# A two-hop graph diffusion: pieces of side work woven between half products instead of whole ones

## The chip, the core and the metric

The kernel runs on one core of a Trainium2 chip. The metric is device time in microseconds. The time of the kernel before is the median of three runs; the profile is of one more execution.

## The reference

Two layers follow each other, each with a pre-norm (`h = relu(layernorm(x))`) and a residual sum. The first is a graph attention over 4096 nodes, 256 features and 4 heads. The second, which the change concerns, is a diffusion of two steps with two ways of mixing nodes:

```python
R = S + I;  R = R / R.sum(-1)              # S is the 4096 x 4096 adjacency
Z = 0;  Xf = X;  Xa = X                    # X is 4096 x 256
for n in range(2):
    q = Xa @ W1.T @ W2.T;  k = Xa @ W3.T   # 64 wide
    probs = softmax(q @ k.T)               # 4096 x 4096
    # per row: keep the largest probs until their sum reaches 0.9, renormalise
    A = probs * mask / (probs * mask).sum(-1)
    Xf = R @ Xf                            # one "hop" over the graph
    Xa = A @ Xa                            # top-p attention
    Z = Z + Xf @ U1[n].T + Xa @ U2[n].T
out = x + layernorm(X + Z)
```

All of it is float32.

## The kernel before

Blocks have 128 nodes, so there are 32 of them (`NB`). After layer 0 (to about 838 us of the span) come, for step 0 and then for step 1: a **hop**, which multiplies by R, and then 32 **attention blocks**, each of some 23 us.

**A hop** is written by the generator `hops` (L509). It goes through 4 passes of 32 products. A product, `graph_products` (L474), takes one block of rows j (256 features, split into a high and a low part, `hl`) and 1024 columns of the adjacency (`ar`) and issues 8 matmuls 512 wide into four accumulator banks (two named acc, two in one mm tile). `fetched` (L450) issues the load of `ar` on SP's queue and, in the second hop, also of the block of rows x, from what the first hop stored in `xf_d`. `split` (L465) makes `hl`: a copy on ACT (L470), a difference on VectorE (L471), and, for blocks on the diagonal, the sum of the identity (L468). Both run `LOOK`, 4, products ahead of PE. At a pass end `drained` (L481) copies the four banks out (L489, two copies on ACT and two on VectorE), then `stored` writes them, and in the first hop four calls of `by_rows` (L496) turn them into rows by PE transposes through a tile named tp, scale them on ACT (L504) and store them in `xf_d`. These calls are taken up one a product from product 2 of the next pass on. After the last pass they are left to the first two attention blocks (`beside`).

**Fill work.** The attention cannot begin before projections, statistics and thresholds are there. That work is cut into pieces by two more generators, and the loop at L1145 advances both by one piece after each product:

- `fills` (L1094) first runs `projections` (L578): for each of 8 groups of 4 blocks a piece of transposes (L595, "T"; ACT copies the result to xs, L596), a piece of matmuls (L601, "M"; VectorE copies, L603) and a piece of transposes (L606, "Q"; ACT and VectorE make kT and qT, L608 to L613). Then come the moments (L619), the largest length km (L625 reduces, L627 transposes), four pieces with statistics (L640 to L645, "sq"), and a chain of small operations on tables (L647 to L690). Then, for blocks 0 to 2, four pieces of logits (L568, into an mm tile) with their exponentials on ACT (L723), called E0 to E2, and a probe of the block before (L730, two ACT passes of 2.0 us each).
- `picks` (L1114) works on VectorE: `halves` (L780) has pieces of one 2.35 us operation (L785), `searching` (L799) pieces of six MAX8 and chains of small ones (L816 to L827).

Tiles tp and mm have two buffers each; one of mm's is held by the accumulators of the running pass. The hop's instructions and the pieces are issued in the order written (`tc.manual_schedule`), on every engine and on SP; the remaining parts are ordered by a scheduler. The first products of the first hop (L534) are issued at the end of layer 0, without pieces. In the second step, X (the attention's result, xa_d) is loaded in 8 transfers, one each second product of the first sixteen.

**Step ends.** `attend` (L926) runs one attention block; `contributed` (L921) multiplies its results by U (the row part `zT`, made from eT by L918, then the hop's part `xf`), `finish` (L1066) adds and, in step 0, stores z_d (L1072). In step 1 `finish_scale` (L1080, on POOL) and `finish_rows` (L1087, three VectorE operations and the store) close a block; the last three are closed after the last block. `repaired` (L1059) is a branch that recomputes rows if a count is above zero; it stands after each step, so between step 0 and hop 2.

Of the kernel before, what the change touches and what calls it, by code (L numbers as in the profile page):

```python
# [26 lines left out]
P = 128  # L27
# [13 lines left out]
G0 = 8  # L41
# [15 lines left out]
def gat_then_top_p_diffusion(  # L57
# [108 lines left out]
    with tc.tile_pool(name="l0", bufs=1) as l0, tc.tile_pool(name="l0s", bufs=2) as l0s, tc.tile_pool(name="l0o", bufs=1) as l0o:  # L166
# [306 lines left out]

        def graph_products(j, acc, ar, hl):  # L474
            for s in range(KC):
                for t in range(2):
                    for c in range(2):
                        nc.tensor.matmul(acc[c][s], hl[:, t, ts(s, P)], ar[:, ts(c, 512)],  # L478
                                         start=(j == 0 and t == 0), stop=(j == NB - 1 and t == 1))

        def drained(hop, p, acc):  # L481

            last = p == PASSES - 1
            room = S.big if last else S.l1e.tile([P, N], F32, name="stage", tag="e1")
            out_ = room[:, :N // 2].rearrange("p (c s b i) -> p c s b i", c=2, s=KC, b=4)
            rows_ = room[:, ds(N // 2, N // 2)].rearrange("p (b d) -> p b d", b=G0)
            for c in (1, 0):
                for s in range(KC):
                    (nc.vector.tensor_copy if s else nc.scalar.copy)(out_[:, c, s].rearrange("p b i -> p (b i)"), acc[c][s])  # L489

            def stored():
                for c in range(2):
                    for s in range(KC):
                        (nc.sync if last else nc.scalar).dma_start(xft_d[hop][ds(p * G0 + 4 * c, 4), :, s, :].rearrange("b p i -> p b i"), out_[:, c, s])

            def by_rows(c, i0):  # L496
                pt = ps2.tile([P, 4, P], F32, name="tp")
                for i in range(2):
                    for s in range(KC):
                        nc.tensor.transpose(pt[:, KC * i + s, :], out_[:, c, s, i0 + i, :], ident)  # L500
                for i in range(2):
                    b = p * G0 + 4 * c + i0 + i
                    row = rows_[:, 4 * c + i0 + i, :]
                    nc.scalar.activation(row, pt[:, ds(KC * i, KC), :].rearrange("p s d -> p (s d)"), AF.Copy,  # L504
                                         scale=rinv[:, b:b + 1])
                    (nc.sync if last else nc.scalar).dma_start(xf_d[b], row)
            return [stored] + ([lambda c=c, i=i: by_rows(c, i) for c in range(2) for i in (0, 2)] if hop + 1 < STEPS else [])

        def hops(hop):  # L509

            fetch, ready, turned = {}, {}, []
            order = [(p, j) for p in range(PASSES) for j in range(NB)]
            for n in range(len(order) + LOOK + 1):
                if n < len(order):
                    fetch[n] = fetched(hop, n, *order[n])
                if 0 < n <= len(order):
                    ready[n - 1] = split(fetch.pop(n - 1))
                if n > LOOK:
                    p, j = order[n - LOOK - 1]
                    if j == 0:  # L520
                        wide = ps2.tile([P, 2, 512], F32, name="mm")
                        acc = [[wide[:, s, :] for s in range(KC)],
                               [ps1.tile([P, 2, D], F32, name="acc").rearrange("p t d -> p (t d)") for s in range(KC)]]
                    graph_products(j, acc, *ready.pop(n - LOOK - 1))
                    if turned and j >= 2:
                        turned.pop(0)()
                    if j == NB - 1:
                        turned = drained(hop, p, acc)
# [4 lines left out]
        with tc.manual_schedule(engines=every | {ET.SP}):  # L533
            for n in range(NB - G0 - LOOK):  # L534
                next(first_hop)
                if later:
                    later.pop(0)()
# [33 lines left out]
    def swapped(src):  # L571
# [4 lines left out]
        return dst  # L576

    def projections(cur, n, G):  # L578

# [10 lines left out]
        for g in range(NB // 4):  # L590
            xs = l1e.tile([P, 3, 4, P], F32, name="xs", tag="e1")
            for k in range(KC):
# [3 lines left out]
                nc.scalar.copy(xs[:, k], pt)  # L596
            yield
            pm = ps2.tile([P, 2, 512], F32, name="mm")
# [4 lines left out]
            nc.vector.tensor_copy(both, pm[:, 0, :].rearrange("p (i m) -> p i m", i=4))  # L603
            yield
            for i in range(4):
# [7 lines left out]
            nc.vector.reduce_sum(lengths[:, ts(g, 4), :], xs[:, 2].rearrange("p i (t m) -> p i t m", t=2), axis=AX.X)  # L613
            yield

# [8 lines left out]
        km = col("km")  # L624
        nc.vector.tensor_reduce(km, lengths[:, :, 0], AX.X, ALU.max)  # L625
        pt = ps2.tile([P, 4, P], F32, name="tp")[:, 0, :]
        nc.tensor.transpose(pt, km.to_broadcast([P, P]), ident)  # L627
        nc.vector.tensor_reduce(km, pt, AX.X, ALU.max)
        yield

# [6 lines left out]
        for g in range(NB // 8):  # L637
# [7 lines left out]
            nc.scalar.copy(mu[:, ts(g, 8)].rearrange("p (h i) -> p h i", h=2), of[:, :, :, 0])  # L645
            yield
        nc.vector.tensor_tensor(var, mu, mu, ALU.mult)  # L647
# [31 lines left out]
        G.kT, G.qT, G.sg = kT, qT, sg  # L679
        yield  # L680

# [98 lines left out]
    def halves(r, op, out_, limit, total):  # L780

        sums = [col(f"{total}{h}", 2) for h in range(2)]
        for h in range(2):
            half = slice(h * (N // 2), (h + 1) * (N // 2))
            nc.vector.scalar_tensor_tensor(out_[:, half], r.e[:, half], limit, r.e[:, half], op, ALU.mult, accum_out=sums[h])  # L785
            yield
        return sums
# [133 lines left out]
    def contributed(r, zT):  # L921
        for i, t in enumerate((zT, r.xf)):
            for k in range(KC):
# [170 lines left out]
    def fills(n, G, found, blocks):  # L1094

        yield from projections(X, n, G)
        for b in range(AHEAD + 1):
            if b < AHEAD:
                r = blocks[b] = began(n, b, G)
            for c in range(4):  # L1100
# [4 lines left out]
                if b > 0:  # L1105
                    first_probe(blocks[b - 1], c)
                    yield
            if b > 0:
# [5 lines left out]
    def picks(n, found, blocks):  # L1114

        for b in range(AHEAD):
            while b not in blocks or not hasattr(blocks[b], "stepped"):
                yield
            r = blocks[b]
            for i in range(6 if b == 0 else 0):  # L1120
                yield
            below = yield from halves(r, ALU.is_le, big, r.c3, "low")
            nc.vector.tensor_tensor(r.low3, below[0], below[1], ALU.add)
            r.thirded = True
            yield from searching(r, found)
            yield
            above = yield from halves(r, ALU.is_ge, r.e, r.t, "kept")
# [3 lines left out]
            r.kept = True  # L1131
            for i in range(3):
                yield

    every = every | {ET.SP}
    for n in range(STEPS):
# [4 lines left out]
        with tc.manual_schedule(engines=every):  # L1141
            pieces = first_hop if n == 0 else hops(n)
            filling, picking = fills(n, G, found, blocks), picks(n, found, blocks)
            count = PASSES * NB - (0 if n else NB - G0 - LOOK)
            for i, _ in enumerate(pieces):  # L1145
                if n > 0 and i % 2 and i < NB // 2:
                    g = i // 2
                    nc.sync.dma_start(cur[:, ts(g, 4), :], xa_d[ts(g, 4)].rearrange("b p d -> p b d"))
                if n == 0 or i > 2:
                    next(filling, None)  # L1150
                    next(picking, None)
                if i == count - 3:
                    first = turn(blocks[0], 0)
# [87 lines left out]
```

## Time and profile before

| | us |
|---|---|
| median of three runs (lowest, highest) | 3015.07 (3013.22, 3017.64) |
| profiled execution | 3014.21 |
| its span | 3012.1 |
| stage of hop 1 in the profile | 839 to 1163 |
| attention blocks of step 0 | 1163 to 1908 |
| end of step 0, branch | 1908 to 1916 |
| hop 2 | 1916 to 2262 |
| attention blocks of step 1 | 2262 to 2998 |
| end | 2998 to 3012 |
| mean granted clock of PE | 0.979 |

PE is TensorE, DVE VectorE, ACT ScalarE, POOL GpSimd, SP the engine whose queue issues most transfers. A row of the timeline has the start and the duration in us, the engine, the line, the operation and its tiles; in square brackets stands the idle time of the engine before it and what ended that. A row of waits has the total, the number and the longest. The granted clock is what the throttle gave PE, 1.0 being full speed. Stages are cut where their first products start, by eye, and PE's pieces overlap their edges by a few us.

### The profile page before, as it was taken

The numbers are of one execution on the slowest core, as the hardware profiler recorded it, in microseconds if no ns is written. First come the engines' busy times: TensorE is split into PE (matmuls) and PEld (weight loads), VectorE is DVE, ScalarE is ACT, GpSimd is POOL, SyncE is SP. The second block draws the span as 40 slices with busy tenths as digits, with TensorE's granted clock in tenths as the row PEclk, the third lists the DMA queues.
The fourth block names the chain that finished last, engine by engine and source line by source line (L and its number), as shares of the span: only waits on it lengthen the run. The fifth ranks groups of instructions, "written<-read, shape, count | busy, mean of one in ns | idle before, by whom it ended". The sixth has DMA issues, their size and how long they took to land. (4 is left out here: it accounts for less than half of the span.)

```text
span 3012.1 us, 51986 instructions
## 1 busy us (share of the span) xinstructions
PE 2848.1 (95%) x19033; PEld 2481.3 (82%) x19033; DVE 2197.5 (73%) x5179; ACT 1921.3 (64%) x3083; POOL 729.9 (24%) x1637
## 2 busy tenths in 40 slices
PE   4699999999999989999999999899889999999998
PEld 3499999999977768788888888777578888888886
DVE  6666877768654391888888888243825999999996
ACT  5777687867733635777777775235217777777772
POOL 3201111111010130323322331001102544454442
PEclk7799999999999999999999999999999999999999
DMA  6859678694466775000000000478881001000100
GB/s 154 177 207 245 183 225 180 241 222 179 172 203 188 215 261 174 23 19 25 19 19 19 23 21 18 152 219 257 277 303 36 24 27 30 25 24 25 32 23 21
DMA packets 181150, 368.13 MB, mean 122 GB/s; under 512 B 17168, under 2 KB 133904, under 8 KB 176784
## 3 DMA queue, kind: packets, MB, share of 16 engines
q1 hardware_dynamic: 129824, 261.55, 26.8%
q0 software_dynamic: 21504, 83.89, 11.7%
q10 hardware_dynamic: 29552, 19.22, 2.1%
q8 instruction: 154, 2.52, 0.3%
q14 instruction: 116, 0.95, 0.1%
HBM read 301.35 MB, written 109.38 MB: 136 GB/s over the span
## 5 line engine op out<-in xcount | busy, mean ns | idle before, releaser
L904 PE MATMUL acc<-X,eT 128*128 128x256 f32 x4096 | 966.0, 381 | 3.6 <-DVE part L1071 3.4
L904 PEld LDWEIGHTS acc<-X,eT 128*128 128x128 f32 x4096 | 743.1, 190 | 101.8 <-ACT eT L898 15.3
L325 PE MATMUL acc<-ut,m 128*128 128x195 bf16 (+1 forms) x8192 | 700.7, 247 | 14.0 <-DVE m L305 8.4
L325 PEld LDWEIGHTS <-m 128*128 128x128 fp8e4 x8192 | 696.4, 97 | 18.2 <-issue 10.0
L723 ACT ACTIVATE e<-mm,nm 128x1024 f32<-128x1024 f32 x256 | 286.6, 1119 | 302.8 <-PE mm L568 287.0
L299 ACT ACTIVATE g<-sr,d_big 128x1024 uint8<-128x1024 f32 x448 | 471.2, 1139 | 5.7 <-DMA s_d<-sT 3.3
L791 DVE SCALAR_TENSOR_TENSOR big<-e,c 128x4096 f32<-128x4096 f32 x58 | 273.0, 4707 | 139.9 <-POOL c L776 61.7
L478 PE MATMUL mm<-ar,hl 128*128 128x512 f32 x844 | 344.0, 408 | 24.2 <-DVE hl L471 9.6
L898 ACT COPY eT<-tp 128x512 f32<-128x512 f32 x512 | 298.9, 584 | 90.7 <-PE tp L896 90.2
L809 DVE MAX8 cand<-big 128x8 f32<-128x228 f32 (+1 forms) x1152 | 348.3, 380 | 0.0
L478 PE MATMUL acc<-ar,hl 128*128 128x512 f32 x844 | 336.7, 399 | 10.9 <-DVE stage L489 5.2
L747 POOL TENSOR_TENSOR sums<-sums 128x2 f32<-128x2 f32 x64 | 14.1, 220 | 1361.2 <-ACT void L730 1361.2
L896 PE MATMUL tp<-ident,e 128*128 128x128 f32 x2048 | 310.4, 274 | 3.3 <-DVE e L833 0.8
L896 PEld LDWEIGHTS tp<-ident,e 128*128 128x128 f32 x2048 | 248.8, 141 | 71.9 <-ACT eT L918 26.5
L305 DVE TENSOR_TENSOR m<-g,ax 128x512 uint32<-128x512 uint32 x256 | 181.4, 709 | 127.5 <-PE acc L325 103.8
L833 DVE SCALAR_TENSOR_TENSOR e<-e,found 128x4096 f32<-128x4096 f32 x58 | 259.6, 4476 | 0.0
L730 ACT ACTIVATE void<-e,c1x 128x2048 int8<-128x2048 f32 x128 | 257.6, 2013 | 1.8 <-issue 1.4
L730 ACT ACTIVATE void<-e,c 128x2048 int8<-128x2048 f32 x128 | 257.5, 2011 | 0.0
L478 PEld LDWEIGHTS mm<-ar,hl 128*128 128x128 f32 x844 | 162.4, 192 | 69.3 <-DVE hl L471 14.8
L568 PE MATMUL mm<-kT,qT 128*128 128x512 f32 x512 | 197.8, 467 | 8.9 <-ACT e L723 7.9
L478 PEld LDWEIGHTS acc<-ar,hl 128*128 128x128 f32 x844 | 162.4, 192 | 44.9 <-DVE stage L489 5.6
L306 DVE TENSOR_TENSOR m<-m,ax 128x512 uint32<-128x512 uint32 x256 | 177.1, 692 | 25.3
(262 smaller groups left out, 3468.6 us busy)
## 6 DMA issues: line engine op xcount, KB each, us to landing
ar<-adj_d SPq DMA_DIRECT2D x211, 512.0 KB, 4.6
adj_d<-ax POOLq DMA_DIRECT2D x32, 2048.0 KB, 6.9
ut<-uv_d SPq DMA_DIRECT2D x60, 784.0 KB, 5.5
aru<-adj_d SPq DMA_DIRECT2D x45, 512.0 KB, 4.5
ax<-in_adj_t_dram POOLq DMA_DIRECT2D x32, 512.0 KB, 15.8
x<-xf_d SPq DMA_DIRECT2D x78, 128.0 KB, 4.7
uv_d<-st ACTq DMA_DIRECT2D x32, 294.0 KB, 4.9
xf<-xft_d SPq DMA_DIRECT2D x64, 128.0 KB, 2.2
```

The source lines that it names most:

```text
L299: nc.scalar.activation(g[:, c, :], shared[k].sr, AF.Relu, scale=BIG, bias=d_big[:, h, j:j + 1])
L325: nc.tensor.matmul(shared[k].acc[i][:, t, :cols], m[t][:, c, ts(i, P)], shared[k].ut[j // QUARTER][:, j % QUARTER, t, :cols], start=(j == ...
L478: nc.tensor.matmul(acc[c][s], hl[:, t, ts(s, P)], ar[:, ts(c, 512)], start=(j == 0 and t == 0), stop=(j == NB - 1 and t == 1))
L568: nc.tensor.matmul(pm[:, h, :], q[t], kT[:, ds(h * (N // 2) + c * 512, 512)], start=(t == 0), stop=(t == 1))
L723: nc.scalar.activation(ev[:, :, c, :], r.pm[c], AF.Exp, bias=r.nm, accum_out=r.sums[:, c // 2, c % 2:c % 2 + 1])
L730: nc.scalar.activation(void, r.e[:, ts(h, N // 2)], (AF.Relu, AF.Sign)[i], bias=r.c1, scale=-1.0, accum_out=r.sums[:, h, 2 + i:3 + i])
L791: nc.vector.scalar_tensor_tensor(big, r.e, r.c3, r.e, ALU.is_le, ALU.mult, accum_out=r.low3)
L809: nc.vector.max(cand[:, s, :], big[:, edges[s]:edges[s + 1]])
L833: nc.vector.scalar_tensor_tensor(r.e, r.e, r.t, r.e, ALU.is_ge, ALU.mult, accum_out=kept)
L896: nc.tensor.transpose(pt[:, i, :], r.e[:, ts(4 * g + i, P)], ident)
L898: nc.scalar.copy(eT, pt)
L904: nc.tensor.matmul(r.acc[:, 0, :], eT[:, i, :], cur[:, j, :], start=(j == 0), stop=(j == NB - 1))
```

## The change

The edit has these parts.

- `graph_products` makes half a product (4 matmuls, one half of the features) a call, and `hops` yields after each half, so the pieces of `fills` and `picks` can stand after each half product. No piece is taken in product 30 of a pass.
- Pieces no longer follow one a slot. `waits(n)` yields n empty slots: pieces of `projections` are 1 slot apart in step 0 and 2 in step 1, exponentials 1, probes 3, `halves` and `searching` 3; the first picks start 10 slots later, and km's transpose stands 3 slots behind its reduction.
- The loads of X stand at each third product of the first 24, instead of each second.
- The first three fetches of hop 2 are written ahead of the last block's closing operations and of the branch, and `hops` takes them over (`early`).
- The `by_rows` of the last pass scale on VectorE instead of ACT.
- `contributed` multiplies the hop's part first, then the row part.
- In step 1 the blocks 29 and 30 are closed inside the last `attend` (`earlier`), and only block 31 after it. In step 0 these calls do nothing.

In numbers of products within the hop, the order of the pieces moves so:

| | before, hop 1 | after, hop 1 | before, hop 2 | after, hop 2 |
|---|---|---|---|---|
| first T | 21 | 20.5 | 4 | 6 |
| a group of T, M, Q | 3 products | 1.5 | 3 | 3 |
| first piece of E0 | 55 | 43 | 38 | 40.5 |
| first probe | about 60 | about 46 | | |
| picks of block 1 | 86–95 | 73–86 | 69–78 | 70.5–83.5 |
| last pick of block 2 | 107 | 100.5 | 90 | 98 |

```diff
-        def graph_products(j, acc, ar, hl):
-            for s in range(KC):
-                for t in range(2):
-                    for c in range(2):
-                        nc.tensor.matmul(acc[c][s], hl[:, t, ts(s, P)], ar[:, ts(c, 512)],
-                                         start=(j == 0 and t == 0), stop=(j == NB - 1 and t == 1))
+        def graph_products(j, s, acc, ar, hl):
+            for t in range(2):
+                for c in range(2):
+                    nc.tensor.matmul(acc[c][s], hl[:, t, ts(s, P)], ar[:, ts(c, 512)],
+                                     start=(j == 0 and t == 0), stop=(j == NB - 1 and t == 1))
...
+                    if last:
+                        nc.vector.tensor_scalar(row, turned_row, rinv[:, b:b + 1], None, ALU.mult)
+                    else:
+                        nc.scalar.activation(row, turned_row, AF.Copy, scale=rinv[:, b:b + 1])
...
-        def hops(hop):
-            fetch, ready, turned = {}, {}, []
+        def hops(hop, early=()):
+            fetch, ready, turned = dict(enumerate(early)), {}, []
             for n in range(len(order) + LOOK + 1):
-                if n < len(order):
+                if len(early) <= n < len(order):
                     fetch[n] = fetched(hop, n, *order[n])
...
-                    graph_products(j, acc, *ready.pop(n - LOOK - 1))
+                    graph_products(j, 0, acc, *ready[n - LOOK - 1])
                     if turned and j >= 2:
                         turned.pop(0)()
+                    yield
+                    graph_products(j, 1, acc, *ready.pop(n - LOOK - 1))
                     if j == NB - 1:
                         turned = drained(hop, p, acc)
                     yield
...
+    def waits(n):
+        for i in range(n):
+            yield
...
-            yield
+            yield from waits(1 + n)          # after T, after M and after Q
...
+        yield from waits(3)                  # between km's reduction and its transpose
...
     def contributed(r, zT):
-        for i, t in enumerate((zT, r.xf)):
+        for i, t in ((1, r.xf), (0, zT)):
...
                 if b > 0:
                     first_probe(blocks[b - 1], c)
-                    yield
+                    yield from waits(3)
...
-            for i in range(6 if b == 0 else 0):
-                yield
+            yield from waits(10 if b == 0 else 0)
             below = yield from halves(r, ALU.is_le, big, r.c3, "low")
...
-            yield from searching(r, found)
-            yield
+            for _ in searching(r, found):
+                yield from waits(3)
+            yield from waits(2)
...
-            pieces = first_hop if n == 0 else hops(n)
+            pieces = first_hop if n == 0 else hops(n, early)
-            count = PASSES * NB - (0 if n else NB - G0 - LOOK)
-            for i, _ in enumerate(pieces):
-                if n > 0 and i % 2 and i < NB // 2:
-                    g = i // 2
+            done = 0 if n else NB - G0 - LOOK
+            for i, _ in enumerate(pieces, 2 * done):
+                if n > 0 and i % 6 == 5 and i // 6 < NB // 4:
+                    g = i // 6
                     nc.sync.dma_start(cur[:, ts(g, 4), :], xa_d[ts(g, 4)].rearrange("b p d -> p b d"))
-                if n == 0 or i > 2:
+                if (n == 0 or i > 10) and i // 2 % NB != NB - 2:
                     next(filling, None)
                     next(picking, None)
...
-            attend(r, cur, blocks[NB - 2], None, {0: beginning})
+            def earlier():
+                for b in range(NB - 3, NB - 1):
+                    finish_scale(blocks[b])
+                for b in range(NB - 3, NB - 1):
+                    finish_rows(blocks[b])
+            attend(r, cur, blocks[NB - 2], None, {0: beginning, 3: earlier})
+            if n + 1 < STEPS:
+                early = [fetched(n + 1, i, *order[i]) for i in range(3)]
             contributed(r, contribute(r))
             finish(r)
-            for b in range(NB - 3, NB):
-                finish_scale(blocks[b])
-            for b in range(NB - 3, NB):
-                finish_rows(blocks[b])
+            finish_scale(r)
+            finish_rows(r)
         repaired(R, cur)
```

More of the change, by code (lines that the diff above doesn't have):

```diff
@@ L503, in by_rows @@
                     row = rows_[:, 4 * c + i0 + i, :]
-                    nc.scalar.activation(row, pt[:, ds(KC * i, KC), :].rearrange("p s d -> p (s d)"), AF.Copy,
-                                         scale=rinv[:, b:b + 1])
+                    turned_row = pt[:, ds(KC * i, KC), :].rearrange("p s d -> p (s d)")
+                    if last:
+                        nc.vector.tensor_scalar(row, turned_row, rinv[:, b:b + 1], None, ALU.mult)
+                    else:
+                        nc.scalar.activation(row, turned_row, AF.Copy, scale=rinv[:, b:b + 1])
                     (nc.sync if last else nc.scalar).dma_start(xf_d[b], row)
             return [stored] + ([lambda c=c, i=i: by_rows(c, i) for c in range(2) for i in (0, 2)] if hop + 1 < STEPS else [])
-        def hops(hop):
-            fetch, ready, turned = {}, {}, []
-            order = [(p, j) for p in range(PASSES) for j in range(NB)]
+        order = [(p, j) for p in range(PASSES) for j in range(NB)]
+        def hops(hop, early=()):
+            fetch, ready, turned = dict(enumerate(early)), {}, []
             for n in range(len(order) + LOOK + 1):
-                if n < len(order):
+                if len(early) <= n < len(order):
                     fetch[n] = fetched(hop, n, *order[n])
@@ L534, in gat_then_top_p_diffusion @@
             for n in range(NB - G0 - LOOK):
+                next(first_hop)
                 next(first_hop)
@@ L603, in projections @@
             nc.vector.tensor_copy(both, pm[:, 0, :].rearrange("p (i m) -> p i m", i=4))
-            yield
+            yield from waits(1 + n)
             for i in range(4):
@@ L613, in projections @@
             nc.vector.reduce_sum(lengths[:, ts(g, 4), :], xs[:, 2].rearrange("p i (t m) -> p i t m", t=2), axis=AX.X)
-            yield
+            yield from waits(1 + n)
         moments = rows.tile([2 * DA, DA + 1], F32, name="moments", tag="q_s", bufs=3)
@@ L645, in projections @@
             nc.scalar.copy(mu[:, ts(g, 8)].rearrange("p (h i) -> p h i", h=2), of[:, :, :, 0])
-            yield
+            yield from waits(2)
         nc.vector.tensor_tensor(var, mu, mu, ALU.mult)
@@ L679, in projections @@
         G.kT, G.qT, G.sg = kT, qT, sg
-        yield
+        yield from waits(2)
     def table(name):
@@ L785, in halves @@
             nc.vector.scalar_tensor_tensor(out_[:, half], r.e[:, half], limit, r.e[:, half], op, ALU.mult, accum_out=sums[h])
-            yield
+            yield from waits(3)
         return sums
@@ L1106, in fills @@
                     first_probe(blocks[b - 1], c)
-                    yield
+                    yield from waits(3)
             if b > 0:
@@ L1119, in picks @@
             r = blocks[b]
-            for i in range(6 if b == 0 else 0):
-                yield
+            yield from waits(10 if b == 0 else 0)
             below = yield from halves(r, ALU.is_le, big, r.c3, "low")
@@ L1124, in picks @@
             r.thirded = True
-            yield from searching(r, found)
-            yield
+            for _ in searching(r, found):
+                yield from waits(3)
+            yield from waits(2)
             above = yield from halves(r, ALU.is_ge, r.e, r.t, "kept")
@@ L1131, in picks @@
             r.kept = True
-            for i in range(3):
-                yield
+            yield
     every = every | {ET.SP}
@@ L1141, in gat_then_top_p_diffusion @@
         with tc.manual_schedule(engines=every):
-            pieces = first_hop if n == 0 else hops(n)
+            pieces = first_hop if n == 0 else hops(n, early)
             filling, picking = fills(n, G, found, blocks), picks(n, found, blocks)
-            count = PASSES * NB - (0 if n else NB - G0 - LOOK)
-            for i, _ in enumerate(pieces):
-                if n > 0 and i % 2 and i < NB // 2:
-                    g = i // 2
+            done = 0 if n else NB - G0 - LOOK
+            for i, _ in enumerate(pieces, 2 * done):
+                if n > 0 and i % 6 == 5 and i // 6 < NB // 4:
+                    g = i // 6
                     nc.sync.dma_start(cur[:, ts(g, 4), :], xa_d[ts(g, 4)].rearrange("b p d -> p b d"))
-                if n == 0 or i > 2:
+                if (n == 0 or i > 10) and i // 2 % NB != NB - 2:
                     next(filling, None)
                     next(picking, None)
-                if i == count - 3:
+                if i == 2 * len(order) - 6:
                     first = turn(blocks[0], 0)
```

## The prediction

> **What bounds the kernel now.** I read the page's first two parts, then the stages by windows, then the waits of PE in the two hops, then the timeline at their worst places.
>
> ```profile
> PE 2848.1 (95%) x19033; PEld 2481.3 (82%) x19033; DVE 2197.5 (73%) x5179; ACT 1921.3 (64%) x3083; POOL 729.9 (24%) x1637
> ```
> PE is the bound. The windows say where it is not busy (columns: PE, PEld, DVE, ACT, POOL busy, granted clock, DMA share, GB/s):
>
> ```profile
> 839.00:1163.00 324.00, 299.37 (x1478) 244.16 (x1479) 172.85 (x448) 128.00 (x274) 42.73 (x85) 0.98 0.73 230
> ...
> 1908.00:1916.00 8.00, 3.01 (x12) 2.15 (x13) 0.91 (x2) 0.45 (x2) 0.00 (x0) 0.87 0.13 41
> 1916.00:2262.00 346.00, 307.65 (x1434) 243.45 (x1433) 157.64 (x388) 112.12 (x230) 21.42 (x51) 0.95 0.81 261
> ...
> 2998.00:3012.00 14.00, 3.11 (x14) 1.89 (x12) 5.02 (x13) 0.85 (x2) 1.00 (x2) 0.79 0.10 33
> ```
> These are hop 1, the branch, hop 2 and the end; the attention stages between have PE busy for 99% and are hardly touched. PE is idle for 24.6 us in hop 1 and 38.4 in hop 2. Matmul starts lie 0.227 us apart in an undisturbed product, so 8 make 1.82 us, half a product 0.91; after some gaps starts lie 0.426 apart. PE's waits, hop 1 then hop 2 (total, times, longest):
>
> ```profile
> PE acc L478 <- DVE stage L489: 5.2, 1, 5.2
> PE mm L568 <- ACT e L723: 4.2, 3, 2.4
> PE mm L478 <- DVE hl L471: 3.8, 3, 2.4
> PE tp L595 <- ACT stage L504: 3.3, 2, 2.3
> ...
> ```
> ```profile
> PE acc L478 <- ACT stage L489: 10.2, 2, 5.4
> PE mm L478 <- DVE hl L471: 5.8, 4, 2.4
> PE mm L478 <- ACT hl L470: 5.1, 7, 1.6
> PE mm L478 <- DVEq L1060: 4.3, 1, 4.3
> PE mm L568 <- ACT e L723: 3.7, 3, 2.3
> PE tp L627 <- DVE km L625: 3.3, 1, 3.3
> PE tp L595 <- DMA X<-xa_d: 2.2, 1, 2.2
> ...
> ```
> The longest are pass ends (L489 copies the accumulators out). Hop 1's third, on DVE and PE:
>
> ```profile
> 1093.27 2.35 DVE L785 SCALAR_TENSOR_TENSOR e<-e,found 128x2048 f32<-128x2048 f32 x1
> ...
> 1095.88 2.35 DVE L785 SCALAR_TENSOR_TENSOR e<-e,found 128x2048 f32<-128x2048 f32 x1
> ...
> 1099.08 0.68 DVE L489 COPY stage<-acc 128x512 f32<-128x512 f32 x1
> ...
> 1099.82 0.80 PE L478 MATMUL acc<-ar,hl 128*128 128x512 f32 x1 [5.21 <-DVE stage L489]
> ```
> Two 2.35 us pieces were queued on DVE ahead of the copy. In hop 2, ACT's splits wait for the rows that hop 1 stored:
>
> ```profile
> ACT hl L470 <- DMA x<-xf_d: 100.0, 52, 6.2
> ```
> And the branch:
>
> ```profile
> 1912.09 0.33 SPq L1072 DMA_DIRECT2D z_d<-part  x1
> ...
> 1915.42 0.77 PE L478 MATMUL mm<-ar,hl 128*128 128x512 f32 x1 [4.34 <-DVEq L1060]
> ```
>
> **The change, hop 1.** PE's instructions stay the same in number. (a) Pass ends: PE waited 0.95, 0.99 and 5.21 us. The last was followed by 6.8 us at granted clock 0.5, which cost 3.4. Sum 10.6. The changed order has no piece in product 30, and a piece between the halves of 31 only at two ends; both queues come nearly empty to the copies. There remain two copies behind each other on each engine (ACT 0.59, DVE 0.68), of which PE waits about 0.8, and 1.4 at the third end: 3.0. Gain 7.5. (b) Turning rows (L500) met a group's transposes (L595) on tile tp: 1.02 and 2.33, and the latter's 3.4 us of half clock cost 1.7. In the new order they fall at products 35.5–38.5 and 67.5–70.5, beside moments and block pieces, which use other tiles. Gain 4.3, with 0.7 kept. (c) Between 1065 and 1091 PE waited 1.17, 0.39, 0.60 and 0.89 for splits queued behind picks of 2.35 (halves) and 1.85 (six MAX8). Picks now come 1.5 products apart instead of 1; in that time DVE has 2.35 and 1.5 splits of 0.42, 3.0 us, against 2.7 of PE's products plus the fills: about even. Gain 1.7. (d) The projections now take a piece each half product. A group is T (0.85), M (1.70), Q (0.40). M needs ACT's two xs copies of 0.58, with only 0.9 us of products between; a split (0.41) may stand before them. I take 0.35 a group, the sort of wait that L601 had in hop 2 (1.9 in 5): 8 groups, +2.8. L640 (sq) had two product starts more to hide its DVE work: +1.2. (e) E0's four logits pieces come a half product apart, and all need the one free mm tile, which ACT gives back after an exponential of 1.12 and 0.2. Before, the waits were 1.68 and 2.36. I take 2.9 for the piece behind the tables' chain (ten small DVE operations of 0.18 and two ACT ones), 1.7 for the half clock that follows, and 0.7 twice: 6.0, +2.0. Hop 1: −7.5 −4.3 −1.7 +2.8 +1.2 +2.0 = −7.5. The turned rows of the last pass go from ACT to DVE, 8 of 0.47; ACT is freed of them in the first attention blocks, while DVE waits there 41 us for these rows' stores anyway: −0.5.
>
> **Transition.** (f) The branch holds everybody until SP has seen the DMAs land that were issued: the z_d store, issued 1912.09, landed 1914.90. The three fetches (512 and 128 KB each) are written ahead of it now. In the trace of before the scheduler had already issued three of them, and a fourth ar, at 1152–1172, off PE's path. So this part brings nothing; moved, they are 1.9 MB on SP's queue between xa_d (1908.11) and z_d, and the barrier waits for them too. At the 261 GB/s of hop 2 that is 7.4 us from about 1908.5, 1916 to 1917.5; the z_d store lands behind. I take +2.4, between 0.8 (they use all queues at once) and 4. The three splits stand behind the branch now: 0.41 and 0.42, +0.5. Transition +2.9.
>
> **Hop 2.** (g) X is loaded each third product instead of each second: the wait of 2.18 and 1.7 of clock behind it shrink to 0.4. −3.5. (h) The wait of L606 at 1945 (2.11, and 1.7 of clock) comes from a split whose x was late; fewer X loads beside it: −1.5 of 3.8. (i) km's reduction and its transpose stand 1.5 products apart: 3.30 becomes 2.3, −1.0; sq +0.8. (j) E0: 1.13, 2.33 and 1.7 of clock become 4.9, as the splits before the chain wait for x here, 1.7, and 0.7 twice: +2.8. (k) The second pass end cost 5.41, 0.69 and 5.1 of clock (10.2 us); the probes (2.0) are gone from before its copies, but the split with x landing at 2113.48 is not: 4.7 and 3.4 remain. −3.1. The third (4.74 at 2190) has no piece in front of it, and stays. (l) From 2135 to 2184 gaps of 0.20 to 2.39 sum to 9.0, behind picks; at 1.5 products apart 3.0 remain: −6.0. Hop 2 without the branch: −11.5.
>
> **End and steps.** `contributed` starts with xf, which needs no eT copy: PE's wait of 0.52 for that copy goes twice, −0.6 to −1.0, of which DVE sees 0.3 each, as its L1075 waits for all eight products. Two of the three blocks' closing rows go into the last `attend`: the last store leaves after one set of L1089–L1091 instead of three, 3 × 0.42 twice is 2.5, less the POOL pair (0.28 and 0.72) that is now uncovered: −1.75.
>
> Sum: −7.5 −0.5 +2.9 −11.5 −0.6 −1.75 = −19. From the profiled 3014.21 (span 3012.1 and 2.1 around it) that is 2995.3; the median of the runs is 0.86 above the profiled one, so 2996.
>
> **A rule and a row.** In this trace gaps of 2.2 to 2.4 us were enough for 3.4 us of half clock (after 1925.42, 1945.13, 2047.27), while 3.30 at 2021 was not. The Trainium skill, "TensorE: Matmul & The Clock Gate", section "HAM oscillation — how this bites in real kernels", puts the danger at idle gaps above about 3.4 us. By it E0's gaps would cost no clock, and the sum would be 3.4 us lower; by the rows, as I have it, they do.
>
> **Rivals.** (1) *Larger gain*: with queues short, waits are gone nearly everywhere. Idle PE of hops and branch is 63 us before; half clock cost 22 (44 us at half). If half of both goes, (63 + 22) / 2 is −42: 2974. For: the gaps are short and depend on queues. Against: hop 2 moves 346 × 261 = 90 MB, and the page's best slice is 303 GB/s, a floor of 298 us; hl waits on x, not on pieces. (2) *Little gain*: structural waits stay, E0 and the barrier eat the rest, (a), (b) and (g) alone survive, at half, −7.7, against +2.9 of (f) and +4.8 of (e) and (j): 0, 3015. (3) *Slower*: the half-product pace. In hop 1 M behind xs and Q behind both (DVE 0.68) have one half product, 0.91, for 1.16 on ACT plus 0.41 of a split. If each group waits 2.5 us and the gap brings 1.7 of half clock, 8 groups cost 34 instead of 2.8: 3027. It decides from 2.7 us a group ((2.8 + 19) / 8). For: ACT stands at 128 of 324 us, bunched. Against: L601 waited at most 0.8 in hop 2. (4) *The loads do not do what they say*: in the sum already, as (f); had they helped, the branch's 4.34 would stay and 2993 come out.
>
> **How the numbers follow.** The measurement tells about 0.2% (6 us) from no change. The forecast has 0.55, spread over −7 to −31 by its unknowns (E0 3, groups 6, barrier 2, picks 6: 17 if all fall on one side, which 12 allows for in most cases); rival 1 0.18, rival 2 0.14, rival 3 0.13. Faster: 0.55, 0.18 and a third of rival 2, 0.77; same 0.09; slower 0.14 (rival 3 and the bad end of 2). The range leaves out the far half of rival 1 and half of rival 3: 2969 to 3019.
>
> **What would show it.** Right: waits of acc L478 on stage L489 in hop 1 under 1.5 each; no tp L595 wait on L504; X<-xa_d gone; PE at branch idle for 6 to 8 us. Wrong: L601 and L606 waits over 2 us in hop 1, with granted clock below 0.95 from 890 to 950; E0's waits over 5 us; the third pass end of hop 2 shorter than 3; the branch no longer than before.

## The result, and the profile after

The changed kernel took 3021.72 us (median of ten runs, 3018.64 to 3027.0) beside 3016.36 for the kernel before in the same ten rounds: ratio 1.002, interval 1.001 to 1.0029. It is slower by about 6 us, at the edge of what can be told, where 20 less were forecast. The profiled execution took 3019.55, its span is 3017.5. Lines have moved: the hop's own by one up, those behind it by six to eleven down. L477 is the products, L488 the copies at pass ends, L507 the scaling of turned rows on ACT, L611 M, L651 the statistics, L574 the logits, L1071 the branch.

Windows over the changed stages (columns as before: PE, PEld, DVE, ACT, POOL busy, granted clock, DMA share, GB/s):

```profile
837.00:1160.00 323.00, 300.86 (x1479) 242.62 (x1480) 172.27 (x447) 128.80 (x273) 43.93 (x85) 0.98 0.71 228
1907.00:1921.00 14.00, 2.42 (x12) 1.61 (x10) 3.06 (x8) 2.06 (x5) 0.00 (x0) 0.79 0.59 201
1921.00:2269.00 348.00, 306.93 (x1434) 243.04 (x1435) 157.41 (x389) 112.28 (x230) 21.61 (x51) 0.96 0.81 260
```
PE is idle for 22 us in hop 1 (24.6 before) and 41 in hop 2 (38.4 before): the waits are about as long as they were. PE's waits of hop 1, and then of the branch and hop 2 (total, times, longest), show that they are different ones:

```profile
PE acc L477 <- DVE stage L488: 4.4, 2, 3.9
...
PE tp L499 <- ACT stage L507: 2.2, 1, 2.2
```
```profile
PE mm L477 <- DVEq L1071: 11.2, 1, 11.2
PE acc L477 <- ACT stage L488: 10.9, 2, 6.2
PE mm L574 <- ACT e L734: 6.7, 3, 4.8
PE mm L477 <- ACT hl L470: 6.0, 7, 1.5
PE mm L651 <- ACT mu L656: 5.0, 2, 3.9
PE mm L611 <- ACT xs L606: 3.5, 7, 1.2
```
In hop 2 the waits for picks (hl L471, 5.8 before) are nearly gone (0.7). The statistics (5.0, before 1.1) and the logits (6.7, before 3.7) took their place.

By stages, a hop from the start of its first product to the end of its last (us, one profile each):

| | before | after | difference | forecast |
|---|---|---|---|---|
| before the first product of hop 1 | 839.5 | 837.4 | −2.1 | 0 |
| hop 1 | 323.6 | 322.3 | −1.3 | −7.5 |
| attention of step 0 and branch | 752.3 | 761.4 | +9.1 | +2.1 |
| hop 2 | 345.0 | 346.2 | +1.2 | −11.5 |
| attention of step 1 and end | 751.8 | 750.0 | −1.8 | −2.05 |

The first row is no effect: no edit lies there, and in the profiles of the kernels below it is 834.6 to 839.9. The differences sum to 5.1, against 5.4 in the spans. Hop 2 in parts: products 0 to 9 took 4.9 less, 32 to 42 took 12.8 more, 64 to 95 took 9.1 less. The 346.2 of hop 2 is a low value: in three kernels below that leave hop 2 as it is here (e2, f2 and g1) it is 350.8 to 352.3.

### The profile page after: what moved, and what is told of

Read it like the earlier page. It is cut to its first block, busy times and chain, and to the rows that moved or that the text cites. A ratio compares the mean times of both kernels' runs of the same rounds, so it can differ in the third digit from the quotient of the medians.

```text
span 3017.5 us, 51984 instructions
## 1 busy us (share of the span) xinstructions
PE 2846.9 (94%) x19033; PEld 2478.0 (82%) x19033; DVE 2199.9 (73%) x5187; ACT 1919.6 (64%) x3075; POOL 730.3 (24%) x1637
## 5 line engine op out<-in xcount | busy, mean ns | idle before, releaser
L477 PE MATMUL mm<-ar,hl 128*128 128x512 f32 x844 | 344.5, 408 | 26.4 <-DVEq L1071 11.2
L477 PE MATMUL acc<-ar,hl 128*128 128x512 f32 x844 | 336.9, 399 | 11.0 <-ACT stage L488 6.2
L477 PEld LDWEIGHTS mm<-ar,hl 128*128 128x128 f32 x844 | 163.1, 193 | 68.3 <-issue 12.7
L574 PE MATMUL mm<-kT,qT 128*128 128x512 f32 x512 | 199.5, 471 | 10.4 <-ACT e L734 9.4
L477 PEld LDWEIGHTS acc<-ar,hl 128*128 128x128 f32 x844 | 162.9, 193 | 45.3 <-ACT stage L488 6.7
```

The source lines that it names most:

```text
L574: nc.tensor.matmul(pm[:, h, :], q[t], kT[:, ds(h * (N // 2) + c * 512, 512)], start=(t == 0), stop=(t == 1))
```

## The experiments

All ratios are to the kernel before, timed in the same rounds; its own median was 3008 to 3016 us from one set of rounds to another, so kernels are compared by ratio. The branch column is PE's idle time there; "third block" is the time from the second attention block's result to the third's, in step 0. Stage times come from one profile each; hop 2 of like kernels differs by up to 6 us from profile to profile. The profiled executions of b2 and k3 took 8 and 6 us more than the medians of these kernels.

| kernel | ratio (95% interval) | hop 1 | branch | third block | hop 2 |
|---|---|---|---|---|---|
| before | 1 | 323.6 | 4.3 | 26.5 | 345.0 |
| after | 1.0020 (1.0010, 1.0029) | 322.3 | 11.2 | 32.3 | 346.2 |
| e1_no_early | 0.9998 (0.9989, 1.0006) | 321.7 | 4.0 | 31.9 | 349.2 |
| e2_rows_act | 1.0037 (1.0024, 1.0049) | 320.1 | 10.7 | 29.4 | 352.3 |
| e3_hold_picks | 1.0009 (0.9999, 1.0019) | 317.9 | 11.3 | 31.3 | 347.2 |
| e5_early_sooner | 1.0015 (1.0006, 1.0024) | 320.8 | 4.1 | 30.7 | 349.2 |
| f1_hop2_old_pace | 1.0015 (1.0005, 1.0024) | 324.3 | 10.7 | 29.2 | 341.8 |
| f2_hop1_old_pace | 1.0021 (1.0011, 1.0032) | 322.5 | 11.3 | 30.5 | 351.0 |
| g1_groups_apart | 1.0017 (1.0007, 1.0028) | 320.5 | 11.4 | 31.9 | 350.8 |
| g2_tables_apart | 1.0022 (1.0012, 1.0033) | 320.4 | 10.9 | 31.9 | 346.7 |
| h1_split_later | 0.9897 (0.9882, 0.9912) | 318.9 | 11.0 | 32.6 | 311.1 |
| h2_before_split_later | 0.9913 (0.9899, 0.9927) | 320.5 | 4.3 | 28.1 | 313.8 |
| b1_best | 0.9846 (0.9831, 0.9860) | 311.9 | 4.2 | 32.6 | 304.8 |
| b2_best_both | 0.9872 (0.9854, 0.9890) | 319.7 | 4.4 | 29.4 | 317.2 |
| k1_split_later_no_early | 0.9873 (0.9857, 0.9890) | 319.3 | 4.1 | 29.3 | 306.8 |
| k2_best_rows_act | 0.9852 (0.9835, 0.9868) | 314.1 | 4.0 | 26.5 | 308.6 |
| k3_best_split_one_later | 0.9878 (0.9861, 0.9894) | 315.3 | 4.3 | 32.5 | 320.0 |

**The loads at the branch**, without them (e1) and with them sooner (e5).

```diff
-                early = [fetched(n + 1, i, *order[i]) for i in range(3)]
+                early = ()                       # e1
...
+            if n + 1 < STEPS:                    # e5: here, ahead of the last block
+                early = [fetched(n + 1, i, *order[i]) for i in range(3)]
             attend(r, cur, blocks[NB - 2], None, {0: beginning, 3: earlier})
```


> Undoes one part of the change: the three fetches of hop 2 are no longer written ahead of the last block's end and of the branch. Theory (the loads hold up the branch: their splits stand in front of ACT's and DVE's branch, and DVE's next instruction comes 2.84 us after its branch): PE's idle time at the branch falls from 11.2 to 4.3 us and the whole time by 6 to 7, to about 3015. Rival (the early loads also pay for hop 2's start, where the changed kernel is 4.9 us faster over products 0 to 9): the branch falls as said, but products 0 to 9 take 3 to 5 us longer, and the time falls by only 2 to 3.

> The three fetches stand ahead of the whole last attention block of step 0 instead of behind it, so that they land some 20 us before the branch. Theory (what costs is loads in flight at the branch, not early loads): PE's idle time at the branch falls from 11.2 to 3 to 4.5 us, the start of hop 2 keeps its gain, and the time falls by 6.5 to 8, to about 3014. Rival (the branch has become longer because there are more instructions of loading in front of it, wherever the loads stand): idle time at the branch stays over 8 us.

Without them the branch is back at 4.0 us and the time at 0.9998, 0.22% below the changed kernel, 6.6 us: the whole excess over the kernel before. Products 0 to 9 of hop 2 keep their gain (4.6), so that came from the pace and the X loads, and the rival falls. With the fetches sooner the branch is 4.1 too: loads in flight at the branch cost, not early ones. But by ratio that kernel is 5 us slower than e1 (3.4 by the medians; the two intervals just touch), although the two profiled spans differ by 0.3; that stays open. The timeline of the changed kernel shows the mechanism:

```profile
1911.15 0.39 SPq L1083 DMA_DIRECT2D z_d<-part  x1
...
1917.22 0.40 ACT L470 CAST hl<-x 128x256 fp32r<-128x256 f32 x1 [1.21 <-SPq L1071]
1917.65 0.42 DVE L471 TENSOR_TENSOR hl<-x,hl 128x256 fp32r<-128x256 f32 x1 [0.38 <-ACT hl L470]
...
1921.17 0.77 PE L477 MATMUL mm<-ar,hl 128*128 128x512 f32 x1 [11.19 <-DVEq L1071]
```
The third fetch's x landed at 1917.19. Its split stands on ACT and DVE ahead of the branch, so DVE came to the branch at 1918.06, and its next instruction was at 1920.90, 2.84 us later. SP, which checks that all transfers have landed, was done at 1919.04. Before, DVE was at the branch at 1912.05 and its next instruction came at 1915.25, 3.20 us later, beside the z_d store's landing at 1914.90. In all seventeen profiles DVE's step over the branch takes 2.79 to 3.21 us, so whatever makes DVE late there makes PE late.

**Rows on ACT again** (e2, and on the best kernel k2).

```diff
-                    if last:
-                        nc.vector.tensor_scalar(row, turned_row, rinv[:, b:b + 1], None, ALU.mult)
-                    else:
-                        nc.scalar.activation(row, turned_row, AF.Copy, scale=rinv[:, b:b + 1])
+                    nc.scalar.activation(row, turned_row, AF.Copy, scale=rinv[:, b:b + 1])
```


> Undoes one part: the last pass's turned rows are scaled on ACT again. Theory (the 5.8 us that the third attention block of step 0 lost come from DVE, which now has these rows in front of its 4.5 us third probe, so that PE waits 5.6 us and then runs at half clock): that block goes from 32.3 to about 27 us, and the time falls by 4 to 5. Rival (PE comes to that place earlier because hop 1's end is different, whichever engine scales the rows): PE still waits over 5 us there, and the time stays within 1.5.

> The best kernel so far (2963), with the last pass's rows scaled on ACT again. Theory (the third attention block's 32 us comes from PE's wait of 5.8 us behind VectorE's third probe, shorter by 2 with these rows on ACT, but still followed by half clock, as in the earlier run of this edit): that block 29 to 30, the time 1 to 3 lower. Rival (what that block gains, the blocks before it lose): time within 1.

PE's wait in the third block goes from 5.6 to 3.4 us in e2 and from 5.8 to 3.35 in k2. In the four kernels with the rows on ACT (before, e2, h2, k2) it is 3.35 to 3.42, in the thirteen with the rows on VectorE 3.65 to 5.97: the wait follows that edit. The block's time follows it less plainly, 32.3 to 29.4 in e2 and 32.6 to 26.5 in k2, because 0, 3.4 or 6.8 us of half clock come with the wait; with the rows on VectorE, too, f1, b2 and k1 have 29.2 to 29.4, with 3.4 us of it. The whole time does not follow: 1.0037 and 0.9852, against 1.0020 and 0.9846. Some is given back. With the rows on ACT the first block, from the hop's end to its result, is 1.5 us longer (23.9 against 22.4), the second 0.6 to 0.7, and in k2 the fourth another 0.7. What is left, 0.7 us in e2 and 3.3 in k2, is less than the intervals can tell. In the changed kernel the place looks so:

```profile
1211.14 4.51 DVE L802 SCALAR_TENSOR_TENSOR big<-e,c 128x4096 f32<-128x4096 f32 x1 [4.02 <-POOL up L776]
...
1216.66 0.76 PE L915 MATMUL acc<-X,eT 128*128 128x256 f32 x1 [5.59 <-DVE part L1082]
```
PE reaches this accumulator at 1211.07, when DVE's probe is only starting, and waits it out; the following 7.4 us have a mean clock of 0.61. In the kernel before, PE came 2.1 us after the probe's start, waited 3.36 and kept full clock.

**Picks held near pass ends** (e3).

```diff
                     next(filling, None)
-                    next(picking, None)
+                    if not NB - 5 <= i // 2 % NB < NB:
+                        next(picking, None)
```


> One more step in the direction of the change: the VectorE picks are held back in the last five products of each pass (27 to 31), the other pieces stay. Theory (the third pass end of hop 1 still costs 3.9 us and some clock because an 4.2 us chain of picks was queued two products ahead of it): the wait for the accumulators' copy there falls under 1.5 us, granted clock there stays at 1.0, and hop 1 takes 3.5 to 5 us less; hop 2's pass ends, which wait for rows of x, stay above 4 us. Rival (DVE has no room, held picks only come later): the pass end gains as said, and the same time is lost in the last pass or at the first attention block, whole time within 1.5.

The wait at hop 1's third pass end, 3.9 us in the changed kernel, is no longer in the list, and products 96 to 100 take 10.1 us instead of 16.9. Hop 1 is 4.4 shorter, the ratio 0.0011 lower (3.3 us, within the intervals). Hop 2's pass ends stay (4.9 and 4.3). The theory holds for the hop; by whole time it fits, but is not shown. What stood in front of the copies in the changed kernel was one piece of the search:

```profile
1091.73 0.31 DVE L827 MAX8 best<-cand 128x8 f32<-128x144 f32 x1
...
1095.49 0.31 DVE L827 MAX8 best<-cand 128x8 f32<-128x144 f32 x1
...
1096.38 0.68 DVE L488 COPY stage<-acc 128x512 f32<-128x512 f32 x1
...
1097.11 0.80 PE L477 MATMUL acc<-ar,hl 128*128 128x512 f32 x1 [3.86 <-DVE stage L488]
```

**The pace in one hop at a time** (f1: hop 2 as before; f2: hop 1 as before).

```diff
-    def waits(n):
-        for i in range(n):
+    def waits(new, old):
+        for i in range(new if S.half else old):
             yield
...
+            S.half = n == 0                      # f1; f2: n == 1
-                if (n == 0 or i > 10) and i // 2 % NB != NB - 2:
+                if ((n == 0 or i > 10) and i // 2 % NB != NB - 2) if S.half else (i % 2 and (n == 0 or i // 2 > 2)):
```
(every `waits(...)` gets the count of before as its second value, and X is loaded at the matching products)

> The changed kernel, with hop 2's pieces and X loads at the pace of the kernel before (one a whole product, none held at product 30); hop 1 and all else stay changed. Theory (in hop 2 the new pace gains about 9 us at its VectorE pieces, products 64 to 96, and 5 at its start, and loses 12 to 13 at products 32 to 43, where statistics and first logits now stand): those three parts go back, and the time stays within 2.5 of the changed kernel's 3021.7. Rival (the new pace in hop 2 is the whole loss): 3014 or less. Rival 2 (it is a gain hidden by the longer branch): 3026 or more.

> The changed kernel, with hop 1's pieces at the pace of the kernel before; hop 2 and all else stay changed. Theory (hop 1's new pace brings 2 to 4 us in the hop and loses 3 to 6 in the third attention block of step 0): that block goes from 32 back to 26 to 28 us, hop 1 takes 2 to 4 us longer, and the time is 1 to 3 lower, 3019 to 3021. Rival (the block's loss comes from the other edits of step 0): the block stays over 31 and the time rises by 2 to 4.

With hop 2's old pace the three parts go back as said (products 32 to 42 take 36.8 us, against 50.4), and hop 2 takes 341.8; the ratio falls by 0.0005 only, within the intervals. The third block does not go back fully with hop 1's old pace (30.5), and the time is unchanged. So, with the splits where they stand, either hop's pace is worth about nothing by time.

**Pieces further apart** (g1: groups in hop 1; g2: statistics and logits in hop 2).

```diff
-            yield from waits(1 + n)              # g1, after T, M and Q
+            yield from waits(2)
...
-            yield from waits(2)                  # g2, after a statistics piece
+            yield from waits(2 + n)
...
-        yield from waits(2)                      # g2, after the chain on tables
+        yield from waits(2 + 6 * n)
...
-                    yield                        # g2, after an exponential
+                    yield from waits(1 + n if b == 0 else 1)
```


> One size changed: hop 1's group pieces (T, M, Q) stand two half products apart instead of one, as in hop 2. Theory (the prediction's term d: M waits for ACT's copies with one half product too little): PE's idle time ahead of M in hop 1 falls from 2.2 us (and an excess of 5.3 over undisturbed starts) under 1.5, and hop 1's products 0 to 127 take 2 to 4 us less. Rival (the eight groups' later end pushes statistics and probes into the next pass end): that gain is lost again before product 96, whole time within 1.5 of 3021.7.

> Hop 2 alone: statistics pieces three half products apart instead of two, four products instead of one between the chain on tables and the first logits, and the first block's logits two half products apart instead of one. Theory (products 32 to 43 lose because these pieces' VectorE steps stand behind splits whose rows of x have not landed, and PE waits for the piece although it has products to do): the waits of the statistics (5.0) and of the logits (6.7) fall to under 2.5 each, and the time falls by 5 to 8. Rival (x is late whatever is woven in, the hop is bound by its transfers): the waits only move to the splits (L470 and L471 as releasers rise by the same), time within 2.

Both miss. In g1 the waits of M vanish from hop 1's list, but Q's (0.5 to 0.7, three times) and a turned row's 2.4 come back; hop 1 is 1.8 shorter and the time the same. In g2 products 32 to 42 do take 15.1 less than in the changed kernel, but 43 to 63, which got the logits, take 17.8 more; products 32 to 63 together take 100.9, against 98.1 in the changed kernel and 84.7 before. The waits of statistics and logits are 3.0 and 8.2. The loss goes along with the pieces, wherever they stand. That left two readings, transfers as the bound or the order of the queues, which the next runs separate.

**Splits later in the order** (h1 on the changed kernel, h2 on the kernel before).

```diff
-                if 0 < n <= len(order):
-                    ready[n - 1] = split(fetch.pop(n - 1))
+                m = n - (3 if hop else 1)
+                if 0 <= m < len(order):
+                    ready[m] = split(fetch.pop(m))
```


> The changed kernel; in hop 2 alone, the split of product n (ACT's and VectorE's step that waits for its rows x) is issued two products later in the order, three products behind its fetch instead of one, and still two ahead of its product. Theory (queue order: fetch n goes out when product n-5 has ended and lands 4.6 us later, but its split stands in ACT's and VectorE's order already beside product n-4, so every piece and every pass end behind it waits for a transfer that PE does not need for four more products; a piece between two halves comes 0.9 us sooner behind that split and waits that much more): ACT's waits for x, the waits of L488's copies, of the statistics and of M fall to less than half, and the time falls by 10 to 20. Rival (hop 2 is bound by the transfers themselves): PE's waits move to the splits, time within 3 of the changed kernel's.

> The same edit in the kernel before: hop 2's splits two products later. Theory (the queue order costs both paces, the half-product one more): the time falls by 7 to 15 against the kernel before, so less than the edit brings in the changed kernel. Rival (only the half-product pace suffers from it): less than 3.

Hop 2 falls from 346.2 to 311.1, and from 345.0 to 313.8 in the kernel before; the ratios are 0.9897 and 0.9913. The theory holds, and its size was too small: the gains are nearly twice the upper ends of the two ranges. The changed kernel gains more (about 37 us against 26), as it said. The same matmuls and the same bytes now move at 289 GB/s; transfers were not the bound. The profile of h1, window of hop 2, then PE's waits and ACT's:

```profile
1919.00:2231.00 312.00, 295.39 (x1433) 240.44 (x1433) 154.63 (x389) 109.55 (x230) 24.14 (x51) 0.98 0.86 289
```
```profile
PE mm L477 <- ACT hl L470: 6.1, 5, 2.7
...
PE mm L575 <- ACT e L735: 1.6, 3, 0.8
PE acc L477 <- ACT stage L488: 1.1, 1, 1.1
```
```profile
ACT hl L470 <- DMA x<-xf_d: 52.6, 28, 5.5
```
ACT's waits for x are half of the 101.3 that they were (52.6); with those for xa, rows of the same kind, they fall from 172.9 to 97.7, not to less than half as the theory had it. Pass ends cost 1.1 instead of 10.9, and M and the statistics have left the list. Where the wait came from is to be seen in the changed kernel's timeline:

```profile
2035.63 0.38 SPq L462 DMA_DIRECT2D xa<-xf_d  x1
...
2041.76 0.41 ACT L470 CAST hl<-xa 128x256 fp32r<-128x256 f32 x1 [2.40 <-DMA xa<-xf_d]
...
2042.69 0.69 DVE L654 TENSOR_TENSOR sq<-mm,e 128x512 f32<-128x512 f32 x1
...
2043.62 0.55 PE L651 MATMUL mm<-moments,qT 128*128 128x65 f32 x3 [3.88 <-ACT mu L656]
```
The row xa was asked for at 2035.63 and landed at 2041.00; PE needs it four products later. But its split stands in DVE's order ahead of sq, and PE waits for sq. (ACT began the split at 2041.76: until 2041.66 it was issuing four stores of the pass end.)

**Together, and the dose** (b1, b2, k1, k3). b1 has e1's, e3's and h1's edits. b2 has e5's instead of e1's and `m = n - 3` in both hops. k1 has e1's and h1's. k3 is b1 with `m = n - (2 if hop else 1)`.

> Three edits on the changed kernel together: no early loads, picks held in the last five products of a pass, hop 2's splits two products later. If the parts add up: 6.5 + 4.7 + 10 to 20 below the changed kernel's 3021.7, that is 2991 to 3001. If the last part brings nothing: about 3010.

> As the one before, but with the fetches ahead of the last attention block instead of not early at all, and the splits two products later in both hops. Theory (in hop 1 a split waits for a transfer only where the identity is added, a quarter of the products, and the copies are from rows in SBUF): hop 1 gains 0 to 3 more; the time is 2989 to 3001. Rival (in hop 1 the split is now too late behind the VectorE picks, with only two products to go): hop 1 loses 3 or more, in waits for L471.

> The changed kernel with hop 2's splits two products later and without the early loads, so that it differs from the second of the kernels before (the old pace with later splits, 2984) by the new pace, the rows on VectorE and the two ends. Theory (the gains that the prediction named are there once the queue order is out of the way): 2971 to 2976, that is 8 to 13 below it. Rival (the new pace is worth nothing in itself): the ends' 2 us alone, 2980 to 2984.

> The best kernel so far (2963), with hop 2's splits one product later instead of two. Theory (a dose: a product with its pieces takes 2.8 us at the filled places, a transfer 4.6 to 5.5, so one product covers about half of the wait): 2970 to 2980, with 0.3 to 0.6 of the gain gone. Rival (any step out of the pieces' way is enough): within 3 of 2963.

b1 is the fastest by ratio: 2963.21 us, 0.9846, below its expected range, because h1's part was (k2 is the same within the intervals). In b2 hop 1 is 7.8 longer than in b1, as its rival said: later splits are bad where nothing is waited for (waits of 2.2 us for L471 stand at 1044 and 1111). Its hop 2 is longer too, by 12.4 in that profile; the whole time is 8 us longer by ratio. k1 is 0.0040 below h2, 12 us: with the queue order out of the way the pace, the rows and the two ends together bring what the theory said, 7.0 of it in hop 2. k3 keeps 33 of the 42 us that b1 has over the sum of e1 and e3 (0.9987, by adding their gains): a dose, with 0.23 of the gain gone, less than the 0.3 to 0.6 that were expected.

## Why the prediction was wrong

The forecast was 2996 with a range to 3019; 3021.72 lies above it, and the sign was wrong. The steps that failed are (f), (a) and above all (i) and (j). One by one:

**(f), the transition: right in kind, too small.** Forecast +2.9 (at most 4.5), measured +6.9 at PE. The failing sentence is that the three splits stand behind the branch. They stand ahead of it and wait for their rows on ACT and DVE, and DVE's 2.84 us at the branch come after that, where the z_d store's landing no longer covers them. The landing itself was well forecast: 1916 to 1917.5, measured 1917.19. e1 shows the price in whole time: 6.6 us. Rival 4, that the loads do not do what they say, was true, and worse than said.

**(a), pass ends of hop 1: the term failed.** Forecast 10.6 to 3.0. The third end still waited 3.86 and ran at a clock of 0.58 over the next 7 us; some 2 us were gained in place of 7.5, and an M piece that waited 1.65 behind the first end's copies took most of that back. "Both queues come nearly empty" was read from which products take pieces, not from how long a piece stays in DVE's queue: the search chain is 4.2 us, more than two products. e3 showed it.

**(b), (c), (d), (e).** The collision on tp went from T to the turned rows themselves (2.2 against 3.3 of waits). (c) was right: 0.8 left of 3.05. In (d) the M pieces took 5.5 us more than before (20.8 against 15.3, each from the start ahead of it to the start behind it) instead of 2.8, with the 1.65 just named. In (e) the logits' waits fell by 1.5 (4.2 to 2.7), where +2.0 was forecast.

**(g), (h): the number right, the reason not.** Products 0 to 9: forecast −5.0, measured −4.9. But the wait for X, 2.18 before, is 2.78 and not 0.4, and Q's wait (1.33, 2.11 before) has in part only moved, to product 11. What these products gained is half clock, 12.1 us of it before and 4.3 after, and that the first group stands two products later. So the match is luck.

**(k), (l): right, the exact match luck.** Products 64 to 95: −9.1 forecast and measured. The second end waited 4.67 (4.7 forecast), the gaps behind it were 3.5 (3.0 forecast). But e2, f2 and g1, with the same hop 2, have −5.6 to −7.4; of the 9.0 us of gaps that the prediction put behind picks, 5.8 stood there, the rest mostly behind ACT's splits; and the third end, said to stay at 4.74, took 6.25.

**(i), (j): the term that undid it.** Forecast +2.6, measured +12.8 over products 32 to 42. The first logits' wait was as forecast (4.9 and 4.8); the statistics' (+0.8) were 5.0 after 1.1. Half clock, of which the sum has one stretch of 3.4 us there both before and after, grew from 3.4 to 13.7 us. Just ahead, km's wait of 3.3 went and the first pass end's of 2.1 came. The prediction priced each wait at its own place. h1, h2 and k3 show one cause behind them: splits that wait for x, ahead of all pieces on two queues. A wait taken from one piece is then found by the next. The trace said so: ACT stood 100.0 us for x in hop 2 before, a line that the prediction quoted and used only to leave the pass ends where they were. With the splits later, products 32 to 42 take 36.0 us in h1, against 50.4, and 32.1 in h2 at the old pace: +3.9, close to the +2.6 that was forecast, once no split stands in the way.

**Rows and ends.** The third block, forecast at −0.5 with all of the rows, lost 5.8: DVE's wait of 41 us was no cover, since DVE and PE meet right behind it. PE's wait there grew by 2.2 us, and 6.8 us of half clock came with it. Its neighbours gave back some, the whole stage less branch was +2.2. The end was right: −1.8 for −2.05.

**The rule.** The limit of about 3.4 us of idle time, which the prediction takes from the Trainium skill, "TensorE: Matmul & The Clock Gate", section "HAM oscillation — how this bites in real kernels", would have put half clock behind longer waits alone. Here waits of 3.35, 3.36, 3.36 and 3.42 us at one place (k2, before, h2, e2) came with 0, 0, 3.4 and 6.8 us of half clock, and 2.12 us at 2024 in the changed kernel with 3.4. So the length of a wait does not decide alone. In all seventeen traces the clock changes only on a grid of 3.413 us: in the kernel before, half clock begins at 862.56, 944.48 and 1098.08, 24 and 45 such steps apart. From 840 to 2300 us, by the profiles' times of PE, all 126 steps at full clock in which PE was idle for 2.0 us or more were followed by half clock, and 2 of the 3358 with less than 1.7 us; in between it was 20 of 38. So in the kernel before the wait of 3.30 at 2021, shared by two steps, went free, and that of 2.11 at 1945, within one step, did not. The same page of the Trainium skill, "TensorE: Matmul & The Clock Gate", has in section "Part 1: The HAM clock gate (the "warmup" mystery)" an idle window that is free-running, which agrees with the grid. (By the cited limit the prediction's sum would have been 1.7 us lower and not 3.4, as the wait of 4.9 that it sets for hop 2 lies above it.)

**Open.** Why e5 is 5 us slower by ratio than e1 with the same branch, and what the rows on VectorE are worth in whole time.

## What to carry to other kernels

Before moving pieces of side work about, look at what stands ahead of them in each in-order queue: a step that waits for a transfer belongs as late as its user allows, not right behind its fetch. A wait that an engine shows at many places with one releaser behind them is one wait, and removing its places one by one moves it. At a branch that waits for all transfers, have none in flight, and no step that waits for one ahead of it on any engine.

## What was not expected of the hardware

The branch has a price of its own on DVE: 2.79 to 3.21 us from its branch instruction to its next one, in every one of the seventeen profiles. Hop 2's transfers ran at 289 GB/s in the mean in h1 and 296 in b1, where the prediction took the 303 of the best slice as a floor to its time; the best slice of b1 has 332. And half clock follows idle time within one step of a fixed grid, so that nearly equal waits at one place differed by 6.8 us of it.
